# Seven block products for half of the key rows, and VectorE instead of ScalarE and GpSimd for one output bank at the end

## The chip, the cores and the metric

The kernel runs on one core of a Trainium2 chip. The core has five engines that run side by side, each through its own list of instructions in order: TensorE (PE in the profile) multiplies matrices out of SBUF into PSUM, VectorE (DVE), ScalarE (ACT) and GpSimd (POOL) work element by element, and SyncE (SP) mostly starts DMAs. PSUM has eight banks of 512 float32 values for each of 128 partitions. An engine that needs another's result waits on a semaphore; those waits are put in by the framework in which the kernel is written, from the tiles that each instruction reads and writes. The metric is the device time of one execution in microseconds (us), the median of several runs.

## The reference

For 16 batches of 512 nodes with 512 features, a graph attention layer in both directions of an adjacency mask:

```python
vcq = concat([v, q], -1)                        # v: 16 x 512 x 512, q is 0 for a node whose row sums to 0
self_feat = vcq @ W_self.T + b_self             # 16 x 512 x 512
output = self_feat
for d in range(2):
    kv = self_feat[:, :20]                      # the first 20 nodes
    qh = (self_feat @ Wq[d].T + bq[d])          # 16 heads of 32
    kh = (kv @ Wk[d].T + bk[d])
    aff = einsum(qh, kh) / sqrt(32)             # each node against 20 keys
    w = softmax(where(mask, aff, NEG) + label_bias)
    output += einsum(w, kv) through Wout[d] + bout[d]
return v + relu(output)
```

All of it is float32.

## The kernel before, in words

**Two stages.** A set-up stage prepares, for all batches together, the keys folded back through the query weights. Then a loop over the 16 batches does the self projection, the scores, the softmax and the output for each. The order of all instructions is written out by hand (`tc.manual_schedule()`), for every engine the order of the program.

**Key rows.** The first 20 nodes of all batches give `kvn`, and `kvD` holds their differences to node 0: four chunks of 128 features, 16 x 19 = 304 columns. `key_rows(d, jc)` (L822 to L835) computes one of eight outputs `khD[:, 4 d + jc]`, 128 rows by 304 columns: 16 matmuls of a 128x32 weight against 304 columns, into one PSUM bank, which VectorE copies to SBUF with the bias added and subtracted again (L835; the two cancel but for rounding, since differences need no bias). Direction d is 0 or 1, jc is 0 to 3. Four outputs (jc 0 and 1) are made before the first burst; the other four (jc 2 and 3) come one ahead of each of bursts 1 to 4.

**Bursts.** `keys(runs)` (L912 to L952) multiplies `khD` with the query weights, in 20 bursts. One burst fills two PSUM tiles of two banks, "s0" and "s1"; ScalarE copies s0 out (L943) and VectorE s1 (L945). There is one buffer of each, so burst n+1 can write only after burst n is copied out. Between two bursts TensorE gets other work from a list, `plan`: pieces of the values `v` and `w` (L887), the bias scores `c` (L860, copied by ScalarE, added to by GpSimd, sent out by GpSimd's own DMA queue, L865 to L871), the row flags `n` (L222) and the seven products `p` of batch 0. `m` is a piece of VectorE work alone (L842: 128x512, both operands in SBUF). After the last m, GpSimd adds two rows into `br_sb` (L1019), which the finished values then read (L900) before they go out (L904). At one finished group of keys GpSimd copies a part into `g0` (L949).

**Other pieces that the change touches.** `weight_sums` (L228 to L234) makes four sums of blocks of the self weights on GpSimd, `ws_s`, used for the first time in the products `p` after burst 13. `row_sums(b)` (L212 to L217) sums the four chunks of x of batch b on GpSimd, three adds of 128x512; `row_flags(b)` (L219) multiplies the result with ones on TensorE. For batch 0 the sums stand ahead of the bursts, for batch 1 behind burst 9; `row_flags(1)` stands behind burst 12. `qwD` (L818) is a small difference on VectorE.

**The end.** For batch 14 (`o`) the output has four PSUM banks. Each is finished either by VectorE in one instruction (`finish`, L585: relu out of PSUM, plus x) or by ScalarE and GpSimd in two (`relieve`, L595, and `residual`, L600). Batch 15 (`b`) is meanwhile in its last softmax: `normal_part` (L478), `turn_part` (L481), the last products (`attend`, L568), then `end` (L610 on VectorE, L612 and L613 on ScalarE and GpSimd) and the last stores (L1339, in SyncE's order behind the stores of batch 14, L617).

Of the kernel before, what the change touches and what calls it, by code (L numbers as in the profile page):

```python
# [13 lines left out]
P = 128  # L14
# [4 lines left out]
def gat_kernel(  # L19
# [47 lines left out]
    def bank(name):  # L67
        return acc["pool"].tile([P, 512], F32, tag="acc", name=name)
# [142 lines left out]

    def row_sums(b):  # L212

        t = rss[b] = load.tile([P, 2, F], F32, tag="xn", name=f"rx{b}")[:, 0]
        nc.gpsimd.tensor_add(t, xs[b][:, 0], xs[b][:, 1])
        for k in range(2, C):
            nc.gpsimd.tensor_add(t, t, xs[b][:, k])  # L217

# [7 lines left out]

    def weight_sums():

        (a11, a12), (a21, a22) = [[ws_v[:, 2 * j : 2 * j + 2, bass.ts(i, F // 2)] for j in range(2)] for i in range(2)]
        s1, s2, s3, s4 = (ws_s[:, i] for i in range(4))  # L230
        nc.gpsimd.tensor_add(s1, a21, a22)
        nc.gpsimd.tensor_sub(s2, s1, a11)
        nc.gpsimd.tensor_sub(s3, a11, a21)
        nc.gpsimd.tensor_sub(s4, a12, s2)  # L234

# [457 lines left out]
    with tc.tile_pool(name="setup", bufs=1) as sp, tc.tile_pool(name="ps_acc", bufs=4, space=PSUM) as acc["pool"]:  # L693
# [16 lines left out]
        kvD = sfp.tile([P, C, N], F32, tag="sf", name="kvD")[:, :, : B * ND]  # L710

        with tc.tile_pool(name="setup_k", bufs=1) as sk:
            xkv = sk.tile([P, C, BM], F32, name="xkv")
# [88 lines left out]
            for fc in range(C):  # L802
# [51 lines left out]
        with tc.tile_pool(name="setup_g", bufs=3) as sg:  # L854
# [99 lines left out]
            def block_product(n):  # L954
# [18 lines left out]
            }  # L973
            plan = "mmvv bvv vvc vvc vvn vvw vw vw wn p p p p p p p".split()

            units = [(fc, hg, d, b) for fc in range(C) for hg in range(C) for d in range(2) for b in range(B)]
            bursts = []
            while units:
# [7 lines left out]
                bursts.append(runs)  # L986
            rest = [(d, hg) for hg in range(C) for d in range(2)]
            first = None
            for r, k in ((0, 0), (1, 0), (0, 1), (1, 1), (2, 0), (2, 1), (0, 2), (1, 2), (3, 0), (3, 1), (2, 2), (3, 2)):
                key_rows(*rest[r], (k,))  # L990
            for r in range(4):
                key_rows(*rest.pop(0), (C - 1,))
            for n, runs in enumerate(bursts):
                for i in range(len(rest)):
                    if (i < 1 and n > 0) or any(fc == 0 and (d, hg) == rest[0] for fc, hg, d, _, _ in runs):
                        key_rows(*rest.pop(0))
                if n in (3, 4):
                    values(*steps["v"].pop(0)[1])
                if n == 0:
# [7 lines left out]
                value_pieces()  # L1007
                if rest:
                    for kind in "mm" if n else ():
                        f, args = steps[kind].pop(0)  # L1010
                        f(*args)
                    continue
                first = n if first is None else first
                for kind in plan[n - first] if n - first < len(plan) else ():
                    f, args = steps[kind].pop(0)
                    f(*args)
                if n == first:
                    for d in range(2):
                        nc.gpsimd.tensor_add(br_sb, br_sb, bo_rows[:, d])  # L1019
                if n > first:  # L1020
                    value_pieces()
                if n == 7:
# [37 lines left out]
    with tc.manual_schedule():  # L1060
# [259 lines left out]
        seed_out(b, 2)  # L1320
        relieve(o, 1)
        turn(b, 0, 1)
# [74 lines left out]
```

## Time and profile before

| | |
|---|---|
| median of 3 runs | 552.3 us (552.06 to 552.35) |
| the profiled execution | 552.61 us, of it 550.8 us from the first to the last instruction (the span) |
| granted TensorE clock | 0.996 of full speed |
| set-up stage | up to 91.8 us, where the scores of batch 0 begin |
| VectorE, ScalarE, GpSimd busy | 87%, 73%, 79% of the span |

A busy time is the union of an engine's instructions on the profile's clock. The chain of work that ended last is followed back from the last instruction: what lies on it sets the time. A row of the timeline gives start, length, engine, line, instruction, output and inputs, and in brackets the idle time ahead of it and what ended it. A float32 matmul of the program leaves two records, so x32 in a row stands for 16 matmuls. Ends of matmuls are modelled, and spans on GpSimd are rough.

### The profile page before, as it was taken

The numbers are of one execution on the slowest core, as the hardware profiler recorded it, in microseconds if no ns is written. First come the engines' busy times: TensorE is split into PE (matmuls) and PEld (weight loads), VectorE is DVE, ScalarE is ACT, GpSimd is POOL, SyncE is SP. The second block draws the span as 40 slices with busy tenths as digits, with TensorE's granted clock in tenths as the row PEclk, the third lists the DMA queues.
The fourth block names the chain that finished last, engine by engine and source line by source line (L and its number), as shares of the span: only waits on it lengthen the run. The fifth ranks groups of instructions, "written<-read, shape, count | busy, mean of one in ns | idle before, by whom it ended". The sixth has DMA issues, their size and how long they took to land.

```text
span 550.8 us, 19622 instructions
## 1 busy us (share of the span) xinstructions
PE 541.0 (98%) x7908; PEld 424.0 (77%) x7908; DVE 480.8 (87%) x707; ACT 404.8 (73%) x1000; POOL 437.0 (79%) x421
## 2 busy tenths in 40 slices
PE   9999999999999999999999999999999999999994
PEld 6554368889787878787888878888878787888882
DVE  0775678888989999999999999999999999999995
ACT  1124445798897979888888888888878787877663
POOL 2636896779979797979798888888888979797575
PEclk9999999999999999999999999999999999999998
DMA  8999999978787887778776758676777677645034
GB/s 303 377 396 343 292 386 336 312 223 249 211 250 208 221 234 221 225 220 236 207 226 188 238 184 232 196 229 192 230 202 224 205 216 200 212 125 163 2 117 154
DMA packets 100530, 126.45 MB, mean 230 GB/s; under 512 B 19592, under 2 KB 68678, under 8 KB 98392
## 3 DMA queue, kind: packets, MB, share of 16 engines
q1 hardware_dynamic: 98696, 121.93, 71.2%
q0 software_dynamic: 1168, 2.23, 1.7%
q8 instruction: 62, 1.02, 0.7%
q10 hardware_dynamic: 576, 1.05, 0.5%
q14 instruction: 28, 0.23, 0.2%
HBM read 86.23 MB, written 40.24 MB: 230 GB/s over the span
## 4 chain that ended last, share of the span: by engine, by line
PE 95%; DVE 3%; ACT 1%; POOL 0%; issue 0%; DVEq 0%
PE ps_f L661 30%; PE ps_a L397 23%; PE ps_c L397 11%; PE ps_d L397 6%; PE ps_o_f L568 5%; PE ps_v L887 3%; PE ps_k L829 3%; PE ps_o_c L568 2%; PE ps_kv L771 1%; PE ps_a L284 1%; PE ps_l L397 1%; PE ps_c L284 1%; PE ps_warm L731 1%; PE ps_e L397 0%; PE ps_d L284 0%
## 5 line engine op out<-in xcount | busy, mean ns | idle before, releaser
L327 ACT ACTIVATE prod<-adj,wb_sb 128x80 f32<-128x80 int32 x330 | 116.0, 429 | 0.0
L536 POOL TENSOR_TENSOR w<-w,sm 128x640 f32<-128x640 f32 x63 | 80.2, 1273 | 33.4 <-DVE sm L532 32.3
L661 PE MATMUL ps_f<-t,ws_s 128*64 128x246 f32 x720 | 80.0, 371 | 0.0
L661 PEld LDWEIGHTS ps_f<-t,ws_s 128*64 128x64 f32 x720 | 51.8, 137 | 18.9
L527 ACT ACTIVATE w<-w 128x640 f32<-128x640 f32 x60 | 43.8, 730 | 18.5 <-DVE w L523 18.5
L544 DVE STREAM_TRANSPOSE wt<-w 128x640 f32<-128x640 f32 x63 | 52.5, 834 | 1.3 <-POOL w L536 1.2
L661 PE MATMUL ps_f<-x,ws_v 128*64 128x246 f32 x480 | 52.4, 371 | 0.0
L531 DVE TENSOR_REDUCE sm<-w 128x32 f32<-128x640 f32 x63 | 51.1, 811 | 1.1 <-ACT w L527 0.9
L522 DVE TENSOR_REDUCE ps_d<-w 128x32 f32<-128x640 f32 x59 | 48.7, 826 | 1.8 <-ACT ps_d L431 0.2
L523 DVE TENSOR_TENSOR w<-w,ps_d 128x640 f32<-128x640 f32 x59 | 48.4, 821 | 2.0
L661 PEld LDWEIGHTS ps_f<-x,ws_v 128*64 128x64 f32 x480 | 34.7, 137 | 13.0
L370 POOL TENSOR_TENSOR k<-g,k 128x608 f32<-128x608 f32 x30 | 44.6, 1488 | 0.0
L397 PEld LDWEIGHTS ps_a<-g,sf 128*64 128x64 f32 x544 | 34.2, 137 | 5.9 <-issue 5.8
L397 PE MATMUL ps_a<-g,sf 128*64 128x152 f32 x544 | 38.6, 295 | 0.0
L338 DVE TENSOR_REDUCE add<-prod 128x80 f32<-128x960 f32 x32 | 36.7, 1148 | 1.5 <-POOL prod L333 1.5
L397 PE MATMUL ps_d<-g,sf 128*64 128x152 f32 x544 | 37.9, 293 | 0.0
L346 ACT COPY both<-add 64x80 f32<-64x80 f32 x128 | 32.6, 255 | 5.7 <-DVE add L338 4.6
L568 PE MATMUL ps_o_c<-wt,vd 32*32 32x256 f32 (+1 forms) x720 | 36.8, 386 | 0.0
L676 POOL TENSOR_TENSOR t<-x,t 128x492 f32<-128x492 f32 x30 | 34.8, 1161 | 1.2
L397 PEld LDWEIGHTS ps_d<-g,sf 128*64 128x64 f32 x544 | 35.3, 137 | 0.2 <-ACT sf L679 0.2
L333 POOL TENSOR_SCALAR prod<-cond 128x80 f32<-128x80 f32 x32 | 18.1, 564 | 21.6 <-DVE cond L332 20.2
L568 PE MATMUL ps_o_f<-wt,vd 32*32 32x256 f32 (+1 forms) x672 | 34.8, 386 | 0.3 <-ACT ps_o_f L555 0.3
(296 smaller groups left out, 1437.9 us busy)
## 6 DMA issues: line engine op xcount, KB each, us to landing
g<-g_d SPq DMA_DIRECT2D x60, 304.0 KB
g_d<-st SPq DMA_DIRECT2D x16, 1064.0 KB
out_T<-o SPq DMA_DIRECT2D x63, 256.0 KB
x<-in_xT SPq DMA_DIRECT2D x56, 256.0 KB
xn<-in_xn SPq DMA_DIRECT2D x48, 256.0 KB
adj<-in_adj SPq DMA_DIRECT2D x52, 220.0 KB
vd<-bd_d SPq DMA_DIRECT2D x64, 64.0 KB
nz<-nz_d SPq DMA_DIRECT2D x14, 256.0 KB
```

The costliest lines, as they stand in the source:

```text
L327: nc.scalar.activation(p[:, :, l], a[:, :, l], AF.Identity, scale=wb_sb[:, l : l + 1])
L338: done["masks"] = nc.vector.tensor_reduce(add, prods.pop((b, h)), AX.X, ALU.add)
L370: done["ksum"] = engine.tensor_sub(to, one, two)
L397: nc.tensor.matmul(slot(g)[bass.ts(p, P // 2), : HL * S].rearrange("p (h m) -> p h m", m=NG)[:, :, 1:], of(k)[:, bass.ds(first + g * P // ...
L522: nc.vector.tensor_reduce(mx, f, AX.X, ALU.max)
L523: done["weigh"] = (engine or nc.vector).tensor_sub(f, f, mx.unsqueeze(2).to_broadcast([P, per, NG]))
L527: done["exp"] = nc.scalar.activation(t, t, AF.Exp)
L531: nc.vector.tensor_reduce(sm, heads(weighs[b, c, l]), AX.X, ALU.add)
L536: done["normal"] = nc.gpsimd.tensor_mul(f, f, smalls.pop((b, c, l)).unsqueeze(2).to_broadcast([P, per, NG]))
L544: done["turn"] = nc.vector.transpose(wts[b][:, c, l], weighs.pop((b, c, l)).rearrange("p g w -> p (g w)"))
L568: nc.tensor.matmul(outsum[b][a][bass.ds(at // 2 * DH, n * DH), bass.ds(c * N // 2 + lo * P, (hi - lo) * P)].rearrange("p (n r) -> p n r", ...
L661: nc.tensor.matmul(parts[b][n in (2, 3, 5)][bass.ts(a, P // 2), bass.ts(i, HN)], lhs, x[:, k], start=False, stop=k == 1, skip_group_check= ...
```

## The change

Three things change in the set-up stage and one at the end.

**Key rows.** Outputs jc 2 and 3 of each direction are no longer made by `key_rows`. They are a matrix of 2 by 2 blocks (two row blocks of 128, two halves of 152 columns), with an inner dimension of two blocks of 256, and are made by seven block products instead of eight, from sums of blocks. A product is four matmuls of a 128x64 weight against 152 columns. Four sums of weight blocks per direction are made by GpSimd (`key_weights`, 128x256 each), four sums of kvD's blocks by VectorE (`kv_sum`, 128x304 each, both operands in SBUF). Two PSUM banks per direction take the products: bank A products 1, 6, 7, 4 in turn, bank B products 2 (columns 0 to 151), 5 and 3 (columns 152 to 303). Between them ScalarE copies A out after 1, 6 and 7 and VectorE adds from B after 2, 7 and 3 and copies A out after 4. The order is 1, 2, 6, 5, 7, 3, 4: five products behind burst 0, six behind burst 1, three behind burst 2.

**Order.** `plan` now counts from burst 0, the m steps stand behind bursts 0 to 3 (two each) rather than 1 to 4, `row_flags(0)` moves from burst 8 to burst 12, in front of `row_flags(1)`. The weight sums of the self projection move on GpSimd from ahead of the bursts to behind bursts 3 to 6, one each; `br_sb` is added to behind burst 3 instead of 4; `qwD` moves behind burst 4; `load_x(1)` is issued behind burst 3, since its home holds the new sums until then. On GpSimd, ahead of the bursts, come the four key sums of direction 0, one add of `row_sums(0)`, the four key sums of direction 1, and the other two adds.

**The end.** Bank 1 of batch 14 is finished by VectorE alone, behind the last `turn_part`, and the stores of chunks 0 and 1 follow there.

```diff
-    def row_sums(b):
+    def row_sums(b, ks=range(1, C)):
...
+        def kv_sum(n):
+            one, two = {
+                1: lambda: (kv_block(0, 1), kv_block(0, 0)), 2: lambda: (kv_block(1, 1), kv_sums[1]),
+                3: lambda: (kv_block(1, 1), kv_block(0, 1)), 4: lambda: (kv_block(1, 0), kv_sums[2]),
+            }[n]()
+            nc.vector.tensor_sub(kv_sums[n], one, two)
...
+        def key_place(d, n):
+            one = n in (2, 3, 5)
+            return key_ps[d, one][:, bass.ts(n != 2, KN) if one else slice(0, KN)]
+        def key_product(d, n):
+            w, x = {
+                1: ((0, 0), kv_block(0, 0)), 2: ((0, 1), kv_block(1, 0)), 3: (4, kv_block(1, 1)),
+                4: ((1, 1), kv_sums[4]), 5: (1, kv_sums[1]), 6: (2, kv_sums[2]), 7: (3, kv_sums[3]),
+            }[n]
+            if n < 3:
+                key_ps[d, n == 2] = bank(f"ps_k{d}_{n}")
+            to, first, last = key_place(d, n), n in (1, 2, 5), n in (2, 3, 4)
+            for k in range(2):
+                for a in range(2):
...
+                    nc.tensor.matmul(
+                        to[bass.ts(a, P // 2)], lhs, x[:, k], start=first and k == 0, stop=last and k == 1,
+                        skip_group_check=True,
+                    )
+        def key_part(d, n):
+            key_product(d, n)
+            f, l = {1: (0, 0), 2: (0, 0), 6: (0, 1), 7: (1, 1), 5: (1, 1), 4: (1, 0), 3: (0, 1)}[n]
+            to, ps, by = khD[:, d * C + 2 + f, bass.ts(l, KN)], key_place(d, n), bk_sb[:, d, 2 + f : 3 + f]
+            if n == 4:
+                nc.vector.tensor_scalar(to, ps, by, by, ALU.add, ALU.subtract)
+            elif n in (1, 6, 7):
+                nc.scalar.activation(to, ps, AF.Identity, bias=by)
+            if n == 7:
+                ps = key_place(d, 5)
+            if n in (2, 3, 7):
+                nc.vector.scalar_tensor_tensor(to, to, by, ps, ALU.subtract, ALU.add)
...
-            load_x(1)
             load_adj(0, 1)
...
-            nc.vector.tensor_sub(qwD, qw[:, :2], qw[:, 2:])
-            weight_sums()
-            row_sums(0)
+            for n in range(1, 5):
+                key_weights(0, n)
+            for n in range(1, 4):
+                kv_sum(n)
+            row_sums(0, range(1, 2))
+            for n in range(1, 5):
+                key_weights(1, n)
+            row_sums(0, range(2, C))
...
             steps = {
+                "k": [(key_part, (d, n)) for d in range(2) for n in (1, 2, 6, 5, 7, 3, 4)],
...
-            plan = "mmvv bvv vvc vvc vvn vvw vw vw wn p p p p p p p".split()
+            plan = "kkkkkmm kkkkkkmm kvkkmm vvmm bvv vvc vvc vv vv vvw vw ww nn p p p p p p p".split()
...
             for r in range(4):
-                key_rows(*rest.pop(0), (C - 1,))
+                key_rows(*rest[r], (C - 1,))
+            kv_sum(4)
             for n, runs in enumerate(bursts):
...
-                if n == first:
+                if n == 3:
+                    load_x(1)
                     for d in range(2):
                         nc.gpsimd.tensor_add(br_sb, br_sb, bo_rows[:, d])
-                if n > first:
-                    value_pieces()
+                value_pieces()
+                if 2 < n < 7:
+                    self_weights(n - 2)
+                if n == 4:
+                    nc.vector.tensor_sub(qwD, qw[:, :2], qw[:, 2:])
...
-        relieve(o, 1)
         turn(b, 0, 1)
         total_part(b, 1, 1, 0)
         normal_part(b, 1, 1, 0, nc.gpsimd)
         residual(o, 2)
         store(o, range(2, 4))
         weigh_plain(b, 1, 1, 1)
-        residual(o, 1)
-        store(o, range(2))
         turn_part(b, 1, 1, 0)
...
         turn_part(b, 1, 1, 1)
+        finish(o, 1)
+        store(o, range(2))
```

More of the change, by code (lines that the diff above doesn't have):

```diff
@@ L210, in load_nz @@
         behind(nc.sync.dma_start(nzs[b], nz_d[b : b + 1].partition_broadcast(P)), ins)
-    def row_sums(b):
[L214 to L217, printed above, removed]
+    def row_sums(b, ks=range(1, C)):
+        if ks[0] == 1 and b not in rss:
+            rss[b] = load.tile([P, 2, F], F32, tag="xn", name=f"rx{b}")[:, 0]
+        t = rss[b]
+        for k in ks:
+            nc.gpsimd.tensor_add(t, xs[b][:, 0] if k == 1 else t, xs[b][:, k])
     def row_flags(b):
@@ L224, in row_flags, with weight_sum, self_weights @@
         nc.vector.tensor_scalar(nzs[b], ps[:, :N], 0.0, None, ALU.not_equal)
[L227 to L234, printed above, removed]
+    def weight_sum(a, to, n):
+        if n == 1:
+            nc.gpsimd.tensor_add(to[1], a(1, 0), a(1, 1))
+        else:
+            nc.gpsimd.tensor_sub(
+                to[n], *{2: lambda: (to[1], a(0, 0)), 3: lambda: (a(0, 0), a(1, 0)), 4: lambda: (a(0, 1), to[2])}[n]()
+            )
+    def self_weights(n):
+        weight_sum(
+            lambda i, j: ws_v[:, 2 * j : 2 * j + 2, bass.ts(i, F // 2)], {i: ws_s[:, i - 1] for i in range(1, 5)}, n
+        )
     def half(l):
@@ L710, in gat_kernel @@
         kvD = sfp.tile([P, C, N], F32, tag="sf", name="kvD")[:, :, : B * ND]
+        KN = B * ND // 2
+        kv_t = load.tile([P, C, N], F32, tag="x1", name="kv_t", bufs=1).rearrange("p c n -> p (c n)")
+        more_t = load.tile([P, 2, S * L], F32, tag="adj", name="wk_t", bufs=3).rearrange("p t w -> p (t w)")
+        rx = load.tile([P, 2, F], F32, tag="xn", name="rx0")
+        rss[0] = rx[:, 0]
+        kv_sums = {
+            n: kv_t[:, bass.ts(n - 1, 2 * KN)].rearrange("p (k n) -> p k n", k=2) for n in range(1, 5)
+        }
@@ new lines, in gat_kernel, with key_weights @@
+        homes = [kv_t[:, bass.ds(8 * KN + i * 2 * P, 2 * P)] for i in range(3)]
+        homes += [more_t[:, bass.ts(i, 2 * P)] for i in range(3)] + [rx[:, 1, bass.ts(i, 2 * P)] for i in range(2)]
+        homes = [t.rearrange("p (k f) -> p k f", k=2) for t in homes]
+        wk_s = [{n: homes[4 * d + n - 1] for n in range(1, 5)} for d in range(2)]
+        def key_weights(d, n):
+            weight_sum(
+                lambda i, j: wk_sb[d][:, 2 * j : 2 * j + 2, bass.ds(F // 2 + i * P, P)], wk_s[d], n
+            )
@@ L986, in gat_kernel @@
                 bursts.append(runs)
-            rest = [(d, hg) for hg in range(C) for d in range(2)]
-            first = None
+            rest = [(d, hg) for hg in range(2) for d in range(2)]
             for r, k in ((0, 0), (1, 0), (0, 1), (1, 1), (2, 0), (2, 1), (0, 2), (1, 2), (3, 0), (3, 1), (2, 2), (3, 2)):
@@ L1007, in gat_kernel @@
                 value_pieces()
[L1008 to L1014, printed above, removed]
+                for kind in plan[n]:
                     f, args = steps[kind].pop(0)
                     f(*args)
-                if n == first:
+                if n == 3:
+                    load_x(1)
                     for d in range(2):
                         nc.gpsimd.tensor_add(br_sb, br_sb, bo_rows[:, d])
-                if n > first:
-                    value_pieces()
+                value_pieces()
[3 more added lines that the diff above has]
+                    nc.vector.tensor_sub(qwD, qw[:, :2], qw[:, 2:])
                 if n == 7:
```

13 lines of the change are left out of this document (8 added, 5 removed).

## The prediction

> **What bounds the kernel now.** I read the page first, for the engine that sets the end, then the chain of work in order of time, for the stage that the change touches.
>
> ```profile
> PE 541.0 (98%) x7908; PEld 424.0 (77%) x7908; DVE 480.8 (87%) x707; ACT 404.8 (73%) x1000; POOL 437.0 (79%) x421
> PE 95%; DVE 3%; ACT 1%; POOL 0%; issue 0%; DVEq 0%
> ```
>
> ```profile
> 17.56 8.39 PE ps_k L829 x128
> ...
> 27.00 2.19 PE ps_k L829 x32
> ...
> 30.31 2.18 PE ps_k L829 x32
> ...
> 37.76 2.18 PE ps_k L829 x32
> ...
> 41.81 1.85 PE ps_v L887 x16
> ...
> 69.98 0.86 PE ps_nz L222 x8
> ...
> 94.04 2.07 PE ps_d L397 x32
> ```
>
> TensorE carries 95% of the chain, and in the set-up stage the pieces follow each other without a gap: a microsecond of matmuls taken out is worth a microsecond, as long as nothing else is late in its place. A new wait of TensorE costs in full too, for nothing behind it has slack to absorb it. Only the last few us hang on other engines.
>
> **The change part by part.**
>
> *Products.* Removed are four key_rows, 2.19 to 2.18 us each (four rows like the two single ones at 27.00 and 37.76): 8.74 us. Added are 14 products of four matmuls, 128x64 by 152. The scores have this very shape: 16 matmuls in 2.07 us, so 0.52 us per product and 7.24 us for 14. **-1.5 us** if TensorE never waits. I see no reason for more than 0.1 either way.
>
> *What the products wait for.* Before, nothing that key_rows wrote was needed at once. Now bank A is copied by ScalarE after product 1 before product 6 may write it, and so on down the order 1, 2, 6, 5, 7, 3, 4. One product lies between, 0.52 us. The copies stand in ScalarE's and VectorE's order behind the burst's own copies:
>
> ```profile
> 24.49 2.13 DVE L835 TENSOR_SCALAR khD<-ps_k,bk_sb 128x304 f32<-128x304 f32 x4 [1.93 <-PE ps_k L829]
> 27.09 1.25 DVE L945 TENSOR_SCALAR st<-s_g(0, 0, 0, 0, 16)1_326 128x608 f32<-128x608 f32 x2 [0.47 <-PE s_g(0, 0, 0, 0, 16)1_326 L921]
> 31.64 0.68 DVE L842 SCALAR_TENSOR_TENSOR bqt<-wq_sb,br_sb 128x512 f32<-128x512 f32 x1
> ```
>
> ```profile
> 27.16 1.07 ACT L943 ACTIVATE st<-s_g(0, 0, 0, 0, 16)0_325 128x608 f32<-128x608 f32 x2 [6.26 <-PE s_g(0, 0, 0, 0, 16)1_326 L921]
> ```
>
> ```profile
> L945 DVE TENSOR_SCALAR st<-_g(0, 0, 1, 10, 16)1_359 128x152 f32<-128x152 f32 x1 | 0.3, 305 | 0.0
> L943 ACT ACTIVATE st<-_g(0, 0, 1, 10, 16)0_358 128x152 f32<-128x152 f32 x1 | 0.3, 302 | 0.0
> ```
>
> A 152-column copy is 0.30 us on either engine. Burst 0 ends at 27.00 as before. ScalarE is done with it at 28.23, copies product 1 until 28.5; product 2 ended at 28.03, so product 6 waits **0.5 us**. The rest of this section runs through: product 5 ends at 29.6, 7 at 30.1, burst 1 (1.13 in the chain, 29.19 to 30.31) at 31.25.
>
> Does bank B make TensorE wait too, although product 5 writes other columns than product 2? The trace has one such case:
>
> ```profile
> 545.21 0.38 ACT L612 ACTIVATE o<-ps_o_s 128x256 f32<-128x256 f32 x1 [2.43 <-PE ps_o_s L568]
> ```
>
> This copy reads columns 0 to 255 of a bank; the matmuls it waited 2.43 us for wrote columns 384 to 511 of it. So the waits go by bank, and I take it that product 5 waits until VectorE has read product 2. The Trainium skill (PSUM — Partial Sum Buffer, PSUM bank collisions raise a hardware error) says to guard PSUM "by bank × quadrant (by bank is the simple version), not by address"; by that rule too product 5 waits, and without it the next term would fall to about 0.6. The row agrees.
>
> *VectorE falls behind.* It gets eight key steps of 0.3 us, and two m's now stand behind burst 0 already, where GpSimd is busy with x sums and key sums:
>
> ```profile
> 18.86 1.04 DVE L813 TENSOR_TENSOR kvD<-kvn 128x304 f32<-128x304 f32 x1
> ```
>
> ```profile
> 18.06 1.51 POOL L231 TENSOR_TENSOR ws_s<-ws_v 128x512 f32<-128x512 f32 x1
> ...
> 22.48 1.27 POOL L234 TENSOR_TENSOR ws_s<-ws_v,ws_s 128x512 f32<-128x512 f32 x1
> 26.56 1.28 POOL L215 TENSOR_TENSOR rx<-x 128x512 f32<-128x512 f32 x1 [2.81 <-DMA x<-in_xT]
> ...
> 31.85 0.64 POOL L949 COPY g<-st 128x152 f32<-128x152 f32 x1 [0.48 <-DVE st L945]
> ...
> 44.52 2.63 POOL L1019 TENSOR_TENSOR br_sb<-br_sb,bo_rows 128x512 f32<-128x512 f32 x2 [0.63 <-DVE bqt L842]
> 48.18 1.69 POOL L904 DMA_DIRECT2D vw_d<-v  x2 [1.03 <-DVE bqw L848]
> 50.90 0.71 POOL L869 TENSOR_TENSOR c<-c,bb_sb 128x320 f32<-128x320 f32 x1 [0.71 <-ACT c L865]
> 59.40 1.23 POOL L871 DMA_DIRECT2D cq_d<-c  x2 [0.94 <-DMA cq_d<-c]
> 67.03 2.63 POOL L217 TENSOR_TENSOR rx<-rx,x 128x512 f32<-128x512 f32 x2
> ```
>
> The VectorE subtraction with both inputs in SBUF took 1.04 us and ended at 19.90, a third of a us after GpSimd's add of 18.06 to 19.57; the GpSimd copy at 31.85 took 0.64 us while the m at 31.64 ran. Each waits until the other's instruction is over; kv_sum(4) and the m's read two SBUF operands too. The Trainium skill (SBUF — State Buffer, Who interferes with whom) says the same: a VectorE instruction with two SBUF inputs contends with a GpSimd instruction that reads SBUF, and the one that comes second blocks. By it the m's of this change wait as reckoned below, and the rows agree.
>
> GpSimd, from 26.56: one x add 1.28, four key sums of about 0.7 (half of 1.27, and a fixed part), two x adds, until about 33.8. VectorE: product 7's step ends at 30.95. The first m takes 0.6 to 31.55; the second waits for an x add that ends at about 32.7 and ends at 33.3. Burst 1's copies follow to 34.6, the steps of products 3, 4 and (direction 1) 2 to 35.45. Only then may product 5 of direction 1 write bank B, which TensorE reached at 33.85: **1.7 us**. Bounds: 0 if neither waits by bank nor by instruction, 0.6 with one of them alone, and 2.8 if kv_sum(4), ready at 26.6 just as the x add starts at 26.56, comes second: then it ends at 28.2 instead of 27.05, burst 0's copies start 1.1 late, and product 5 of direction 0 waits 0.7 besides. The two starts are equal by the rows; I take the cheaper.
>
> *Third section.* Burst 2 starts at 36.05, behind product 5, and ends at 37.1. ScalarE copies it until 38.3, then product 7 until 38.6, VectorE's step until 38.95; TensorE has product 7 and one v (half of 1.85), until 38.5, and then product 3 waits: **0.5 us**. Burst 3 ends at 41.25. VectorE has the steps of products 3 and 4 until 40.45, two m's until 41.65, burst 3's copies until 42.95 and the last two m's until 44.2.
>
> *GpSimd behind burst 3.* Before, it went from br_sb at 44.52 to the end of row_sums(1) at 69.66, 25.1 us, and row_flags(1) used that on TensorE at 69.98: no slack. Now four weight sums of 1.27 come in between, 5.1 us, while the idle times in the rows above (1.03, 0.71 and 0.94) can fill: 27.6 us. From 44.2 that is 71.8, row_flags(1) at 71.9. TensorE, with -1.5 and 2.7 of waits, would be there at 71.2: **0.7 us** more. Bounds: 0, if more idle fills, and 1.5, if the wait of 0.94 stays.
>
> What moves at no cost: load_x(1), used behind burst 9 only; it leaves SyncE's queue earlier and re-enters it behind the stores of burst 3. If it were late, row_sums(1) would be, one for one. qwD and row_flags(0) need nothing earlier. Key sums of direction 0 and kv_sums 1 to 3 lie under the 8.39 us of key_rows, where VectorE idled 1.93.
>
> *The end.*
>
> ```profile
> 15.41 0.49 DVE L805 TENSOR_TENSOR qp<-nzk,qw 128x320 f32<-128x320 f32 x1
> ...
> 536.41 0.63 DVE L585 SCALAR_TENSOR_TENSOR o<-ps_o_c,x 128x512 f32<-128x512 f32 x1
> ...
> 542.05 1.48 DVE L478 TENSOR_TENSOR w<-w,sm 128x320 f32<-128x320 f32 x1
> 543.56 0.51 DVE L481 STREAM_TRANSPOSE wt<-w 128x320 f32<-128x320 f32 x1
> ```
>
> ```profile
> 540.69 2.49 POOL L600 TENSOR_TENSOR o<-o,x 128x512 f32<-128x512 f32 x2
> ```
>
> The normalisation at 542.05 waits for GpSimd's second residual, the one that goes: 0.49 instead of 1.48, and the last turn ends at 543.1 instead of 544.07. `finish` (0.63) lies under the last matmuls and ends at 543.75. So the arithmetic ends 1.0 us sooner, but the two stores that started at 543.20 now start at 543.8, and the final stores queue behind them:
>
> ```profile
> 541.99 0.81 SPq L617 DMA_DIRECT2D out_T<-o  x2
> 543.20 0.83 SPq L617 DMA_DIRECT2D out_T<-o  x2
> 544.68 0.33 SPq L1339 DMA_DIRECT2D out_T<-o  x1
> 546.11 0.99 SPq L1339 DMA_DIRECT2D out_T<-o  x2
> ```
>
> ```profile
> 542.00:543.00 1.00, 0.00 (x0) 0.00 (x0) 0.96 (x2) 0.78 (x2) 1.00 (x1) 1.00 0.18 70
> 546.00:547.00 1.00, 0.00 (x0) 0.00 (x0) 0.74 (x3) 0.00 (x0) 0.39 (x1) 0.70 0.30 113
> 547.00:548.00 1.00, 0.00 (x0) 0.00 (x0) 0.00 (x0) 0.00 (x0) 0.00 (x0) 0.50 1.03 385
> ```
>
> Issue at 541.99, data from 542.82 (share 0.18): 0.83 later. A 256 KB chunk at 385 GB/s is 0.68. Before there was a hole around 546.5 (share 0.30), and the last three chunks ended at 549.0. Now six chunks run on end from 543.8 + 0.83: to 548.7. **-0.3 us**, between 0 and -1.0.
>
> *Sum:* -1.5 + 0.5 + 1.7 + 0.5 + 0.7 - 0.3 = **+1.6 us**. The profiled execution, 552.61 (span 550.8 and 1.8 around it), becomes 554.2; it stands 0.3 above the median, so the median goes from 552.3 to **553.9 us**, 0.3% slower.
>
> **The rivals.**
>
> *The expensive order:* kv_sum(4) comes second to the x add. 1.15 more in the early waits; with the POOL term at its middle, 555.1 us. For it: equal starts in the rows; against: VectorE needs to be only 0.02 us earlier. 15%.
>
> *The cover nearly holds:* m's and x adds take turns without loss, or product 5 need not wait; the early waits are 0.5, 0 to 0.6 and 0.5, and GpSimd costs 0.4 as more idle time fills. With -1.5 and -0.3 that is 551.9 to 552.5, call it 552.2. For it: before, six m's stood among the same bursts, and the chain shows no wait. Against it: GpSimd was nearly idle then. 29%.
>
> *Not slower, but faster:* the small copies slip in ahead, because ScalarE and VectorE finish a burst's copies before the product behind it ends. This decides at product 6 of direction 0: it pays if the burst's copies of 1.07 shrink below the 1.0 us of products 1 and 2, and if the m's don't meet GpSimd. Then -1.5, 0.3 of waits and the end at up to -1.0: 550.4. Against it: 1.07 and 0.30 are measured, and 1.37 doesn't fit into 1.04. That the products don't save what they should (0.52 each) belongs on the other side; the score's shape is the same, so I give it nothing of its own. 15%.
>
> **How the numbers follow.** Forecast 553.9 us with 41%, the expensive order 555.1 with 15%, the near cover 552.2 with 29%, the fast case 550.4 with 15%. A measurement of this kernel can tell about 0.2%, 1.1 us, from no change: the bounds are 551.2 and 553.4. The forecast and the expensive order lie above (0.56), the near cover within (0.29), the fast case below (0.15). The range runs from 550.9, which takes in the upper half of the fast case, to 555.6, the expensive order with the POOL term at nearly its upper bound. The forecast's own range, slower alone, is 553.0 to 554.8.
>
> **What would show it.** Products: 14 groups of 0.52 us in the chain, or not. The waits: pieces of ps_k in the chain longer than 0.52 or idle before product 6 (direction 0), 5 and 3 (direction 1), with ScalarE and VectorE as releasers; m's of over 1 us while GpSimd adds. GpSimd: the end of row_sums(1) against row_flags(1), which should start on its heels. The end: L478 at 0.49, and a DMA share of 1 without a hole to the last store. I am wrong if burst 5 starts before 44.6 (43.67 before, plus one more v) or if row_flags(1) is reached with GpSimd long done.

## The result, and the profile after

| | before | after |
|---|---|---|
| median of 6 runs each, side by side | 552.22 us (551.97 to 552.35) | 562.74 us (559.26 to 563.19) |
| ratio, 95% interval | | 1.0181 [1.0168, 1.0194] |
| the profiled execution | 552.61 us, span 550.8 | 562.0 us, span 560.2 |
| granted TensorE clock | 0.996 | 0.986 |

The change costs 10.5 us. I had forecast 553.9 us, and a range that ended at 555.6: the direction was right and the size was not. The page of the changed kernel, its engine totals and its chain by engine:

```profile
PE 543.9 (97%) x7892; PEld 428.3 (76%) x7892; DVE 483.7 (86%) x716; ACT 406.4 (73%) x1005; POOL 440.8 (79%) x428
PE 82%; DMA 5%; DVE 5%; POOL 4%; issue 1%; SPq 1%; ACT 1%; DVEq 0%; POOLq 0%
```

TensorE held 95% of the chain and now holds 82%; transfers, VectorE and GpSimd, on which nothing but the last few us hung, share most of the rest. (About 2 points of the DMA's 5 are no loss: the chain follows product 6's wait of 0.46 us to GpSimd's add of x and from there to the load of x, where e8 below has the same 0.46 put down to ScalarE's copy.) Its *busy* time rose by 2.9 us all the same, although the change was to take work from it. Both are explained in the set-up stage. First where the time went: TensorE's rows at four marks, the starts of burst 0, burst 3, burst 12, and of a group of the first scores (ps_d), before and then after.

```profile
25.89 0.53 PE L921 MATMUL s_g(0, 0, 0, 0, 16)0_325<-khD,wq_sb 32*128 32x304 f32 x2
36.51 0.30 PE L921 MATMUL _g(0, 2, 0, 14, 16)0_449<-khD,wq_sb 32*128 32x38 f32 x2
67.17 0.65 PE L921 MATMUL s_g(2, 1, 1, 4, 16)0_807<-khD,wq_sb 32*128 32x228 f32 x4
```

```profile
25.07 0.53 PE L1000 MATMUL s_g(0, 0, 0, 0, 16)0_332<-khD,wq_sb 32*128 32x304 f32 x2
42.65 0.30 PE L1000 MATMUL _g(0, 2, 0, 14, 16)0_480<-khD,wq_sb 32*128 32x38 f32 x2
71.18 0.65 PE L1000 MATMUL s_g(2, 1, 1, 4, 16)0_824<-khD,wq_sb 32*128 32x228 f32 x4
```

The chain of the changed kernel has the fourth mark at 103.77; before it was at 94.04, shown with the prediction:

```profile
103.77 2.07 PE ps_d L403 x32
```

Before, one key row of 2.18 us still stood behind burst 3; I count it into the first stretch, where the products that replace it stand.

| stretch, us | before | after | difference |
|---|---|---|---|
| burst 0 to burst 3 | 10.62 + 2.18 = 12.80 | 17.58 | +4.78 |
| burst 3 to burst 12 | 30.66 - 2.18 = 28.48 | 28.53 | +0.05 |
| burst 12 to the first scores | 26.87 | 32.59 | +5.72 |
| first scores to the end of the span | 456.76 | 456.43 | -0.33 |

The sum is +10.22. (Burst 0 itself starts anywhere from 24.6 to 26.1 in the profiles of this study, with the edit or without: the first loads vary.) So there are two losses, of about 5 us each, and the small gain at the end that I had reckoned.

**The first loss.** The timeline of the changed kernel, VectorE's two m's behind burst 0, GpSimd's x adds, and TensorE's products that waited:

```profile
30.63 1.81 DVE L921 SCALAR_TENSOR_TENSOR bqt<-wq_sb,br_sb 128x512 f32<-128x512 f32 x1
...
32.37 1.75 DVE L921 SCALAR_TENSOR_TENSOR bqt<-wq_sb,br_sb 128x512 f32<-128x512 f32 x1
...
35.91 0.36 DVE L786 SCALAR_TENSOR_TENSOR khD<-khD,bk_sb,ps_k 128x152 f32<-128x152 f32 x1
```

```profile
30.61 2.96 POOL L218 TENSOR_TENSOR rx<-rx,x 128x512 f32<-128x512 f32 x2
```

```profile
27.84 2.04 PE L769 MATMUL ps_k<-kv_t 128*64 128x152 f32 x24 [0.46 <-POOL rx L218]
...
36.32 1.28 PE L769 MATMUL ps_k<-kv_t,wk_t 128*64 128x152 f32 x8 [2.29 <-DVE khD L786]
...
41.46 0.74 PE L769 MATMUL ps_k<-kvD,rx 128*64 128x152 f32 x8 [0.28 <-DVE khD L786]
```

GpSimd's add starts at 30.61 and VectorE's m at 30.63: the m loses by 0.02 us and lasts 1.81 instead of 0.68, and the next one loses again. VectorE's step for product 2 of direction 1 is done at 36.27, and product 5, which writes other columns of the same bank, starts at 36.32, 2.29 us late. Then something that no waiting row shows. Stretches of 4 us of the changed kernel; the columns are the length, TensorE's busy time, the granted clock, the DMA share and GB/s:

```profile
36.00:40.00 4.00, 3.68 (x32) 0.58 0.56 219
...
72.00:76.00 4.00, 0.56 (x6) 0.69 0.91 345
76.00:80.00 4.00, 4.00 (x28) 0.50 0.85 306
```

After both long waits TensorE runs at half its clock for some us. The product behind the wait lasts 1.28 instead of 0.74, burst 2 ends 1.92 us after it starts (37.53 to 39.45) where burst 0 takes 1.05 (25.07 to 26.12). In the last row TensorE is "busy" all 4 us with 28 records; before, the same 4 us of the span held 52. That is how busy time can rise while work falls.

**The second loss.** TensorE's row at burst 12, VectorE's copy of the fourth value tile, GpSimd's transfer of the second tile's rows, and the piece of the chain between them:

```profile
75.44 0.75 PE L1000 MATMUL s_g(2, 1, 1, 4, 16)1_825<-khD,wq_sb 32*128 32x228 f32 x2 [3.60 <-DVE st L1024]
```

```profile
72.32 0.69 DVE L979 SCALAR_TENSOR_TENSOR v<-br_sb,ps_v 128x512 f32<-128x512 f32 x1 [4.40 <-DMA vw_d<-v]
```

```profile
52.72 1.28 POOL L233 TENSOR_TENSOR ws_s<-ws_s,ws_v 128x512 f32<-128x512 f32 x1
...
59.99 2.51 POOL L950 DMA_DIRECT2D cq_d<-c  x4 [0.29 <-POOL c L948]
62.49 1.48 POOL L983 DMA_DIRECT2D vw_d<-v  x2
```

```profile
63.38 8.81 DMA vw_d<-v
```

The five value tiles share a pair of buffers (`msk`, tag "full"). The fourth must wait until the second one's rows have landed; those go out at 62.49, and the chain has 8.81 us for it. Behind the waiting copy in VectorE's queue stand the copies of burst 11, so burst 12 cannot write its banks: 3.60 us, and half the clock behind it (`row_flags` 3.35 us for both batches, where one took 0.86 in the chain before).

The end went as reckoned: the normalisation lasts 0.49, the last stores are issued from 554.32, and the transfers run on, with a dip (share 0.76) where there was a hole (0.30). A row of VectorE and one of SyncE, and two stretches of 1 us (the last columns are the clock, the DMA share and GB/s):

```profile
551.76 0.49 DVE L484 TENSOR_TENSOR w<-w,sm 128x320 f32<-128x320 f32 x1
```

```profile
554.32 1.52 SPq L1411 DMA_DIRECT2D out_T<-o  x3
```

```profile
554.00:555.00 1.00, 0.00 (x0) 0.00 (x0) 0.95 (x3) 0.32 (x1) 0.73 (x2) 0.88 0.76 283
...
557.00:558.00 1.00, 0.00 (x0) 0.00 (x0) 0.00 (x0) 0.00 (x0) 0.00 (x0) 0.50 1.03 383
```

### The profile page after: what moved, and what is told of

Read it like the earlier page. It is cut to its first block, busy times and chain, and to the rows that moved or that the text cites. A ratio compares the mean times of both kernels' runs of the same rounds, so it can differ in the third digit from the quotient of the medians.

```text
span 560.2 us, 19616 instructions
## 1 busy us (share of the span) xinstructions
PE 543.9 (97%) x7892; PEld 428.3 (76%) x7892; DVE 483.7 (86%) x716; ACT 406.4 (73%) x1005; POOL 440.8 (79%) x428
## 3 DMA queue, kind: packets, MB, share of 16 engines
q10 hardware_dynamic: 576, 1.05, 0.5%
## 4 chain that ended last, share of the span: by engine, by line
PE 82%; DMA 5%; DVE 5%; POOL 4%; issue 1%; SPq 1%; ACT 1%; DVEq 0%; POOLq 0%
PE ps_f L667 29%; PE ps_a L403 22%; PE ps_c L403 10%; PE ps_d L403 6%; PE ps_o_f L574 5%; DMA x<-in_xT 2%; DMA vw_d<-v 2%; PE ps_o_c L574 1%; DMA ws_q<-in_wsT 1%; PE ps_k L769 1%; PE ps_a L290 1%; POOL cq_d L950 1%; DVE st L1024 1%; PE ps_l L403 1%; PE ps_c L290 1%
## 5 line engine op out<-in xcount | busy, mean ns | idle before, releaser
L376 POOL TENSOR_TENSOR k<-g,k 128x608 f32<-128x608 f32 x30 | 44.6, 1485 | 0.0
```

The lines of the kernel that those rows point to most:

```text
L376: done["ksum"] = engine.tensor_sub(to, one, two)
```

## The experiments

Theory at the start: the time is lost in queues. VectorE's m's meet GpSimd's x adds, and GpSimd's weight sums between the bursts delay the value rows. Rival: the products themselves, their banks and their order, cost it. Line numbers shift by a few between kernels. "Stretches" below are those of the table above, as differences to before; each is read from one profiled execution, while the time is the median of several.

**e4_end_only (e4): the end alone**, put into the kernel before.

```diff
-        relieve(o, 1)
...
-        residual(o, 1)
-        store(o, range(2))
...
         turn_part(b, 1, 1, 1)
+        finish(o, 1)
+        store(o, range(2))
```

> The kernel before with the change at its end alone. Theory (the final stores then run on end): 0.3 us less than before, 551.9 us, with the normalisation on VectorE at 0.49 us. Rival (the end follows the arithmetic): 1.0 us less, 551.2 us.

Measured 551.58 us (11 runs) against 552.09, ratio 0.9992 [0.9983, 1.0000]. In its profile the stretch from the first scores to the end is 456.43, the same -0.33 as in the changed kernel. The end is worth 0.3 to 0.5 us, and the loss is all in the set-up stage.

**e2_adds_later (e2): the x adds later.** Two of the three x adds of batch 0 go behind burst 1, away from the two m's behind burst 0.

```diff
-            row_sums(0, range(2, C))
...
+                if n == 1:
+                    row_sums(0, range(2, C))
```

> The changed kernel with the last two adds of the x sums of batch 0 moved on GpSimd behind burst 1, where it idles. Theory: the two m's behind burst 0 then take 0.68 us each instead of 1.75, product 5 of direction 1 waits 0 to 0.3 us instead of 2.3, and the clock stays at 1.0 between 36 and 40 us: about 3.8 us less, 558.9 us; the wait of burst 12 stays. Rival (the banks): product 5 waits about as long, since it waits for VectorE's steps in any case, 562 us.

Measured 558.71 us, ratio 1.0115 [1.0097, 1.0134]: 4.0 less than the change. The m behind burst 0 and product 5:

```profile
30.36 0.78 DVE L920 SCALAR_TENSOR_TENSOR bqt<-wq_sb,br_sb 128x512 f32<-128x512 f32 x1
```

```profile
33.95 0.74 PE L769 MATMUL ps_k<-kv_t,wk_t 128*64 128x152 f32 x8 [0.20 <-DVE khD L786]
```

Without the add beside them the two m's behind burst 0 last as before, product 5 waits 0.20, and the clock stays at 1.00. (A later m, at 33.82, now lasts 1.23 beside the moved adds; it stands behind the step for which product 5 waits.) Burst 12 still waits 3.29. The two losses are separate.

**e7_fill (e7): work for the idle TensorE.** Is the low clock a consequence of idling? Four products whose result isn't used go ahead of product 5 of direction 1, in free columns of bank A.

```diff
+            if (d, n) == (1, 5):
+                for k in range(4):
+                    nc.tensor.matmul(
+                        key_ps[d, False][:, 2 * KN : 3 * KN], wk_sb[d][:, k, :P], kvD[:, k, :KN], start=k == 0, stop=k == 3,
+                        skip_group_check=True,
+                    )
```

> The changed kernel with four more products of 128x128 by 152 columns (their result is not used) in unused columns of the first key bank, ahead of product 5 of direction 1, where TensorE waits 2.29 us. They need about 0.3 us of each 0.43 us estimate, 1.7 us in all, and so lie within the wait. My theory (the half clock from 36 to 40 us comes from the idle time): product 5 starts when it did, the clock stays at 1.00 there, and burst 2 takes 1.05 us instead of 1.95: about 561 us, 1.6 us less than the changed kernel. If the low clock has another cause: 562.7, no change, or up to 1.7 us more where the products do not fit in the wait.

Measured 559.95 us (558.87 to 560.48), ratio 1.0136 [1.0120, 1.0153], 2.8 less than the change. The added products, product 5, and the stretch that had 0.58:

```profile
35.10 1.30 PE L765 MATMUL ps_k<-kvD,wk 128*128 128x152 f32 x8 [0.48 <-ACT khD L788]
36.68 0.74 PE L775 MATMUL ps_k<-kv_t,wk_t 128*64 128x152 f32 x8 [0.28 <-DVE khD L792]
```

```profile
36.00:40.00 4.00, 3.72 (x44) 1.00 0.67 264
```

Counted from burst 0, product 5 starts 0.24 earlier than in the change (11.01 against 11.25 us); burst 3 comes 1.67 earlier. The 1.4 us between are the clock: more work, less time. The other 0.9 us of this profile lie behind burst 12 and were not expected.

**e1_sums_early (e1): the weight sums ahead of the bursts**, where they stood before.

```diff
+            for n in range(1, 5):
+                self_weights(n)
             row_sums(0, range(1, 2))
...
-                if 2 < n < 7:
-                    self_weights(n - 2)
```

> The changed kernel with the four sums of the self weights put back ahead of the bursts on GpSimd, behind the key sums of direction 0, where GpSimd idles from 20.9 to 26.5 us. Theory (two queues): the wait of burst 12 (3.6 us, and about 2.5 us of low clock behind it) comes from GpSimd sending the second value piece 8 us later than before, because three weight sums stand in front of it. It should go: 562.7 - 6 = about 556.7 us, burst 12 without idle time, clock 1.0 there. Rival (the block products themselves cost what they cost, through their banks and their order): no GpSimd order matters, 562 to 563 us.

Measured 558.37 us, ratio 1.0111 [1.0094, 1.0128]. It lies 1.7 over what I expected: burst 12 still waits 1.56. The second value rows go out at 59.45 instead of 62.49, not at 54.41 as before the change. Nor is all of its gain in the right place: the stretches are +3.24, -0.09 and +3.28. The third is 2.4 less than in the change, which I put down to the weight sums; the first is 1.5 less, because product 5 waits 2.20 us without the low clock behind it, which this edit cannot be credited with.

**e3_both (e3): both.** The edits of e1 and e2 together.

> Both moves of the two runs before. Theory: the sum of both, about 9.8 us less: 552 to 553 us, no faster than the kernel before by more than 0.5 us. Rival: 561 us or more.

Measured 556.67 us, ratio 1.0078 [1.0064, 1.0092]: a miss by some 4 us. The first stretch is +1.15, the second -0.09, but the third still +4.51. Burst 12 waits 1.89 and burst 13 0.81, with the low clock between them. GpSimd's order of work accounts for part, not for all of the second loss. In this kernel the second bias-score step's transfers stand ahead of the second value rows, which I blamed next.

**e5_both_c_late (e5) and e6_c_late (e6): that step a burst later**, in e3 and in the changed kernel.

```diff
-            plan = "kkkkkmm kkkkkkmm kvkkmm vvmm bvv vvc vvc vv vv vvw vw ww nn p p p p p p p".split()
+            plan = "kkkkkmm kkkkkkmm kvkkmm vvmm bvv vvc vv vvc vv vvw vw ww nn p p p p p p p".split()
```

> The kernel e3_both with one step moved: the second of the two bias-score steps is issued one burst later, so that GpSimd's two transfers of the first values' rows go out between the four transfers of the first step and the four of the second, as before the change. My theory: what is left of the loss in e3_both is GpSimd's limit on transfers in flight, which delays the first value rows to 58.4 us; with the transfers in the old order they go out at about 54 us, VectorE's wait for the value buffer and TensorE's waits of 1.89 and 0.81 us at bursts 12 and 13 go, and with them about 1.7 us of low clock: 556.7 - 2.7 - 1.7 = about 552.3 us, between 551.5 and 553.5. Rival (the block products themselves cost it, the waits later are a consequence that only moves): 556 us or more, with the waits at another burst.

> The changed kernel with only that step moved (second bias-score step one burst later); the weight sums stay between the bursts and the x adds ahead of them. It isolates the order of GpSimd's transfers. My theory: the transfers are issued in the old order, but the weight sums still stand in GpSimd's queue ahead of them, so that burst 12 waits about 1 to 2 us instead of 3.6: 562.7 - 3 to 4 (with some of the low clock) = about 559 us. If the weight sums alone were the cause of the late value rows: no change, 562.7. If the order alone were it: 558 or less.

e5 measured 559.38 us, ratio 1.0129 [1.0114, 1.0144], *worse* than e3 by 2.7; e6 561.63 (559.65 to 563.07), ratio 1.0169 [1.0142, 1.0196], 1.1 under the change and within the spread of its runs. My theory of the transfers' order fell, and e5 showed why. The second rows do go out at 52.81 now, and burst 12 doesn't wait. But the fifth value tile does, and TensorE at burst 13 (the second fence is from the list of waits: us in total, times, the longest):

```profile
73.68 0.69 DVE L980 SCALAR_TENSOR_TENSOR v<-br_sb,ps_v 128x512 f32<-128x512 f32 x1 [6.56 <-DMA vw_d<-v]
```

```profile
PE _g(2, 2, 0, 14, 16)1_858 L1001 <- DVE st L1025: 4.5, 1, 4.5
```

The wait went on to the next tile, whose buffer is the third one's. (In e6, too, burst 12 waits only 0.91, and burst 13 2.05.) Whichever rows are late, the next copy but one pays. So I looked at *when* the copies are asked for. In the kernel before, the fourth tile was finished behind burst 11 and the fifth behind burst 12; the new `plan` finishes them behind 10 and 11. The kernel before was already at the limit, in a row that I hadn't read:

```profile
71.92 0.69 DVE L900 SCALAR_TENSOR_TENSOR v<-br_sb,ps_v 128x512 f32<-128x512 f32 x1 [0.32 <-DMA vw_d<-v]
```

New theory: the pair of buffers is asked for one burst, some 3 us, before it comes free.

**e8_both_old_plan (e8) and e9_old_plan (e9): the old order over the bursts**, in e3 and in the changed kernel. It is the old one for the fourth and fifth value tile, the bias scores and the row flags; two value pieces stand behind burst 3 and two behind burst 9, where the kernel before had one and three.

```diff
-            plan = "kkkkkmm kkkkkkmm kvkkmm vvmm bvv vvc vvc vv vv vvw vw ww nn p p p p p p p".split()
+            plan = "kkkkkmm kkkkkkmm kvkkmm vvmm bvv vv vvc vvc vvn vw vw vw wn p p p p p p p".split()
```

> The kernel e3_both with the order of the value products, bias scores and row flags over the bursts as it was before the change: the fourth value tile is finished behind burst 11 and the fifth behind burst 12 (the change has 10 and 11), the second bias-score step follows the second value tile, one row-flag step goes to burst 8. My theory now, after e5_both_c_late, where VectorE's fifth value copy waits 6.56 us for the third tile's transfer: the five value tiles share two buffers, a transfer needs 8 to 10 us from its issue to its landing, and the change asks for the fourth and fifth tile one burst (about 3 us) earlier than the buffers come free. With the old order the waits at bursts 12 and 13 (1.89 and 0.81) and the low clock behind them (about 1.7 us) go: 556.7 - 4.4 = about 552.3, between 551 and 553.5. Rival (the transfers' queue is late whatever the order, because the GpSimd work ahead of it is later): 555 us or more.

> The changed kernel with only that order put back; the weight sums stay between the bursts, the x adds ahead of them. My theory: the waits at burst 12 and 13 and their low clock (about 6 us together) go or shrink to below 1 us, the wait at product 5 with its low clock (2.29 and up to 1.65) stays: 562.7 - 5 to 6 = 557 us. If the weight sums on GpSimd are a cause of their own, about half of it stays: 559 to 560. If neither: 562.7.

e9 measured 555.59 us, ratio 1.0059 [1.0046, 1.0072]: with this one line the time is 7.1 of the 10.5 us lower, though the weight sums stay where they were. e8 measured 554.21, ratio 1.0033 [1.0020, 1.0046]: 8.5 of them, short of the 552.3 I expected. The stretches of e9 are +2.38, +1.37 and +0.63 (e8: +1.24, +0.90, +0.06). The third is what the line was to do, 5.1 us less than in the change; but the second is 1.3 more, so that the line itself is worth about 3.8. The first, 2.4 less, it cannot have done, for nothing differs there: in e9's profile the race of the m's went another way. Its first m behind burst 0, and GpSimd's adds:

```profile
30.44 0.86 DVE L921 SCALAR_TENSOR_TENSOR bqt<-wq_sb,br_sb 128x512 f32<-128x512 f32 x1
```

```profile
30.71 3.41 POOL L218 TENSOR_TENSOR rx<-rx,x 128x512 f32<-128x512 f32 x2
```

The m came 0.27 us ahead of the add and lasted 0.86; product 5 waited 1.34 and the clock stayed at 1.00. In e6, whose code is alike there, it waited 1.21: there the add began 1.1 us ahead of the m and was nearly over. Counted from the start of burst 0, GpSimd's first add of x began after 0.14 us in e6, 1.45 in the change and 1.74 in e9. So part of the first loss hangs on when the first x arrives.

**e10_buffers (e10): more buffers, the order untouched.** The third and fourth value tile get places of their own in two unused rows of the tile of bo.

```diff
-                    v = msk.tile([P, H * S], F32, tag="full", name=f"v{t}{ds[0]}")[:, :F]
+                    v = bo_rows[:, 2 + ds[0]] if t == 1 else msk.tile([P, H * S], F32, tag="full", name=f"v{t}{ds[0]}")[:, :F]
```

> The changed kernel, its order untouched, with the third and fourth value tile in two places of their own (the two unused rows of the tile of bo) instead of the shared pair of buffers, so that no value copy waits for another tile's transfer to land. My theory (the pair of buffers, asked for a burst too early, makes VectorE wait and TensorE with it): the 3.6 us at burst 12 and the low clock behind it go, about 5.7 us from burst 12 to the loop; a wait of up to 1 us of the second row-flag step for GpSimd's row sums, which ended at 74.4, may come in its place: 557 to 558. Rival (the order over the bursts matters by something else, for example by which engine copies when): 560 or more.

Measured 556.68 us (554.49 to 557.81; the profiled execution is the slowest), ratio 1.0069 [1.0051, 1.0087], 6.1 less than the change. This separates the buffers from everything else in the order. From its list of waits (us in total, times, the longest):

```profile
PE s_g(2, 1, 1, 4, 16)1_823 L1000 <- DVE st L1024: 0.9, 1, 0.9
```

The stretches are +4.78, +0.06 and +0.67: the first loss is untouched to the hundredth, the second falls from 5.72 to 0.67. No value copy waits for a transfer any more.

**e11_order (e11) and e12_order_buffers (e12): the products spread.** e11 is e8 with a burst between products 2 and 6; e12 has the places of e10 as well.

```diff
-            plan = "kkkkkmm kkkkkkmm kvkkmm vvmm bvv vv vvc vvc vvn vw vw vw wn p p p p p p p".split()
+            plan = "kkmm kkkkkkkmm kkkvkkmm vvmm bvv vv vvc vvc vvn vw vw vw wn p p p p p p p".split()
```

> The kernel e8_both_old_plan with the block products spread so that a burst stands between product 2 and product 6 of each direction (two products behind burst 0, seven behind burst 1, five behind burst 2). Expected by what the products' rows show: the wait of 0.46 us at product 6 of direction 0 goes, and with it some 0.2 us in which the last product drains; 554.2 - 0.7 = 553.5, between 553 and 554.5. If the products wait for VectorE elsewhere instead: 554 or more.

> The kernel e11_order with the two places for the value tiles as well. Expected: the waits at bursts 10 and 12 (0.75 of stretch and 0.30 in e8_both_old_plan) shrink, 553.5 - 0.5 to 1 = 552.7; whether it is level with the kernel before (552.2) tells whether anything of the block products is gained when no wait is left. If the stretch at burst 10 has another cause: 553.5.

e11 measured 554.54 us, ratio 1.0045 [1.0033, 1.0057], e12 555.03 (553.54 to 557.28), ratio 1.0056 [1.0037, 1.0075]: no gain over e8's 554.21 in either. The wait at product 6 shrinks to 0.25, and product 3 of direction 0 waits 0.98 in e11 instead; the first stretch is +2.26 in e11 and +2.28 in e12, 1 us more than in e8. The waits of the products moved on among themselves. The second stretch is long in e12 as well (+0.88), so it isn't the buffers. The rows of e8 point to VectorE. Burst 10 starts at 61.69, but the half of it that writes s1 starts 0.80 later, just behind the end of VectorE's copy of burst 9's s1 (62.34):

```profile
62.49 0.53 PE L1001 MATMUL s_g(2, 0, 0, 0, 16)1_749<-khD,wq_sb 32*128 32x304 f32 x2
```

```profile
61.14 1.20 DVE L1025 TENSOR_SCALAR st<-s_g(1, 3, 0, 7, 16)1_719 128x342 f32<-128x342 f32 x2
```

With two value pieces behind burst 9, TensorE is there one piece earlier than in the kernel before, which had three. No run tests this reading.

**What the products cost when nothing else is in the way.** e8's TensorE rows, from the end of burst 0 to burst 3:

```profile
25.98 1.25 PE L769 MATMUL ps_k<-kvD,wk 128*64 128x152 f32 x16
27.70 2.04 PE L769 MATMUL ps_k<-kv_t 128*64 128x152 f32 x24 [0.46 <-ACT khD L782]
29.67 0.37 PE L1001 MATMUL _g(0, 0, 1, 10, 16)0_380<-khD,wq_sb 32*128 32x114 f32 x2
...
30.80 0.74 PE L769 MATMUL ps_k<-kvD,wk_t 128*64 128x152 f32 x8
31.36 0.69 PE L769 MATMUL ps_k<-kv_t,wk 128*64 128x152 f32 x8
31.88 1.20 PE L769 MATMUL ps_k<-kvD,wk 128*64 128x152 f32 x16
33.15 0.74 PE L769 MATMUL ps_k<-kv_t,wk_t 128*64 128x152 f32 x8
34.09 0.74 PE L769 MATMUL ps_k<-kv_t,wk_t 128*64 128x152 f32 x8 [0.20 <-DVE khD L786]
34.76 0.46 PE L1001 MATMUL s_g(0, 1, 1, 4, 16)0_441<-khD,wq_sb 32*128 32x228 f32 x2
35.80 0.74 PE L769 MATMUL ps_k<-kv_t,rx 128*64 128x152 f32 x8
...
37.80 0.74 PE L769 MATMUL ps_k<-kvD,rx 128*64 128x152 f32 x8 [0.26 <-DVE khD L786]
...
38.98 0.30 PE L1001 MATMUL _g(0, 2, 0, 14, 16)0_484<-khD,wq_sb 32*128 32x38 f32 x2
```

The pieces between bursts run from 25.98 to 29.67, 30.80 to 34.76 and 35.80 to 38.98: 10.83 us. Less one v (0.96, half of the 1.92 that two take) and the idle 0.46, 0.20 and 0.26, the 14 products take **8.95 us**, 0.64 each. Four key rows took 8.74. Start to start, a product with another behind it takes 0.52 to 0.57 (30.80, 31.36, 31.88); ahead of a wait it takes longer: product 6 of direction 1 starts at 33.15 and the wait of 0.20 begins at 33.89, 0.74 later. So each wait costs its idle time and, by these rows, about 0.2 more that counts as busy. With the 0.92 of idle time, the products in e8 cost 1.1 us more than the key rows: so much of the rival at the start holds.

## Why the prediction went wrong, step by step

Its sum was +1.6; the stretches say +10.2.

- **Products, -1.5: wrong, +0.2 (measured in e8).** 0.52 us came from 16 score matmuls in a row without a wait; that is the price of a product inside a run. With waits between, it is 0.64. I gave it 0.1 either way and dismissed "the products don't save what they should".
- **Product 6, 0.5: right (0.46). Product 3, 0.5: 0.28.** The copies of 0.30 us and the order of queues were read rightly.
- **Product 5, 1.7: the mechanism right, the size not.** It waited by bank, for a copy of other columns, and the m's waited for whole GpSimd instructions. I gave the first m a length of 0.6; it lost as well, by 0.02 us, and the wait was 2.29. My own figures said so: 26.56 + 1.28 + 4 x 0.7 lets the two x adds start at 30.64 (they did at 30.61), ahead of the m that I had at 30.95; they end at 33.3 by the same sum, and I wrote 33.8. The rival "expensive order" had such a coin toss, at kv_sum(4); the coin lay at the m. Another 1.4 us came from the low clock behind the idle time (e7), for which the sum had no term.
- **GpSimd behind burst 3, 0.7 at row_flags(1): the wrong place.** GpSimd's work was as long as reckoned (27.49 us from br_sb to the end of the row sums, 27.6 in the sum), but TensorE came later still: the row sums were done at 74.43, and row_flags began at 77.38. This was one of the two signs that I had named for being wrong. The other, burst 5 ahead of 44.6, did not occur: it started at 48.60.
- **The step that failed** is the list "What moves at no cost". It names load_x(1), qwD, row_flags(0) and the sums, and leaves out the value tiles, which the new `plan` finishes a burst earlier. I followed GpSimd's delay only to the row flags, and not to the transfers in the same queue and the buffer that they free. The term is 5.7 us in the third stretch, and three runs show it: e10 takes it away with buffers alone (0.67 is left), e9 with the order alone (0.63, though 1.3 come back in the second stretch), e5 moves it to the next tile.
- **The end, -0.3: right, -0.33** in the changed kernel and in e4; it is the only part that pays.

A closing sum for the changed kernel: products +0.2, idle 0.46 + 2.29 + 0.28, clock 1.4, together 4.6 of the 4.78 in the first stretch; 3.60 idle at burst 12 and most of the other 2.1 at half the clock in the third; -0.33 at the end. Of the kernels tried, only e4 lies below the kernel before, by 0.08%, with an interval that touches 1.

## What to carry to other kernels

A rotating buffer that is emptied by a DMA has a due time: issue to landing, counted back from the next copy but one. Before moving a step by even one slot, look for its `<-DMA` wait in the old trace; 0.3 us of it means that there is no slack left. And price a short piece of work by a row in which it stands alone between waits: what fourteen products gain in a run of matmuls they lose when some wait for a copy of the one before.

## What the runs showed of the hardware

**The clock falls after a short idle time, but not always.** 2.29 us idle in the changed kernel and 2.28 in e10 halved it (in both it is 0.57 to 0.58 from 36 to 40 us), while 2.20 us in e1 did not:

```profile
36.10 0.74 PE L769 MATMUL ps_k<-kv_t,wk_t 128*64 128x152 f32 x8 [2.20 <-DVE khD L786]
```

```profile
36.00:40.00 4.00, 3.63 (x43) 1.00 0.66 264
```

Yet in the same execution of e1 a wait of 1.56 us at burst 12 was followed by half the clock (from its list of waits, and the stretch behind it):

```profile
PE s_g(2, 1, 1, 4, 16)1_825 L1002 <- DVE st L1026: 1.6, 1, 1.6
```

```profile
72.00:76.00 4.00, 4.00 (x28) 0.57 1.02 392
```

The Trainium skill (TensorE: Matmul & The Clock Gate, Part 1: The HAM clock gate) says that TensorE goes to half clock after at least one idle window of about 3.4 us, and that the windows run free of the kernel. The rows agree that a wait of much the same length may fall on either side; they do not agree on the length, since 1.56 us sufficed.

**Transfers of 5 to 256 KB from GpSimd's queue took 6 to 9 us to land** in this stage, where the DMA engines are nearly full (share 0.97 to 1.03 from 52 to 72 us). The list of DMA issues of the changed kernel from 50 to 80 us, with KB each and the median us from issue to landing:

```profile
vw_d<-v POOLq DMA_DIRECT2D x2, 256.0 KB, 8.2
...
cq_d<-c POOLq DMA_DIRECT2D x8, 5.0 KB, 5.9
```

The fit that the Trainium skill gives (DMA: Bandwidth & Descriptors, Anatomy of one DMA) gives an estimate of about 2.0 us for 5 KB; here it took three times as long.

**A GpSimd add that starts 0.02 us ahead of the m** cost the m 1.1 us in the changed kernel (1.81 instead of 0.68); with the m 0.27 us ahead (e9) it lasted 0.86, against 0.78 in e2 with no add beside it.
